# Layer 1 of a four-layer graph network: the next layers' weights are loaded and folded inside its first block, and the next block's first edge weights are written ahead of the evictions

## The chip, the cores and the metric

The kernel runs on one core of a Trainium2 chip. The metric is the device time of one execution in microseconds (us), as a median of runs. The profile is one further execution, taken by the hardware profiler; its times are counted from the first instruction of the span.

The engines are called PE (TensorE, matrix multiplication), DVE (VectorE), ACT (ScalarE), POOL (GpSimd) and SP (SyncE, which here only issues DMAs). DMAs are issued from SP, from ACT and from POOL.

## The reference

Four graph layers over the same 3327 nodes with 256 features and one dense 0/1 adjacency matrix. Each is followed by a residual and a layer norm. The change concerns layer 1 and its transition to layer 2:

```python
def _L1_gnn_ref(h, adj, W, a):
    Wh = h @ W.T
    a1, a2 = (a[:F_out], a[F_out:])
    s1 = Wh @ a1
    s2 = Wh @ a2
    e = jax.nn.leaky_relu(s1[:, None] + s2[None, :], negative_slope=LEAKY_SLOPE)
    e = jnp.where(adj == 0, NEG_INF, e)
    attention = jax.nn.softmax(e, axis=1)
    return attention @ Wh
...
x = _layernorm(x + _L0_gnn_ref(x, adj, ...), axis=-1)
x = _layernorm(x + _L1_gnn_ref(x, adj, L1_gnn_W, L1_gnn_a), axis=-1)
x = _layernorm(x + _L2_gnn_ref(x, adj, L2_gnn_W_fc, L2_gnn_b_fc, L2_gnn_w_att, L2_gnn_b_att), axis=-1)
x = _layernorm(x + _L3_gnn_ref(L3_gnn_t, x, adj, L3_gnn_W1, ...), axis=-1)
```

Layer 2 is a layer of the same kind without the leaky step, and with a bias. Layer 3 is two layers of four heads each (here l3a and l3b).

## The kernel before

**Tiles and blocks.** The nodes are 26 tiles of 128 rows (the last has 127). The target nodes are dealt into four blocks of 7, 7, 6 and 6 tiles. A layer walks over the blocks b, and in each block over all 26 source tiles j. For each j it needs the transposed adjacency of tile j against the block (`at_i`, 128 x 896 int32, 448 KB, in the first two blocks), the features of tile j (`feat`) and the edge weights `e` (L1629: max(rate, q) * adjacency, one DVE instruction). Then PE multiplies `e` with `feat` into one PSUM bank for each target tile of the block (L1723, seven matmuls a step, 257 columns: 256 sums and the softmax's denominator). Seven of the eight banks are accumulators; bank 7 serves everything else (projections, transposes).

**Layer 1, a step.** `adjacent` (L1644) takes the adjacency tile that was asked for, copies it as bf16 on ACT (L1656) and stores the copy in memory (`at_d`, from ACT's queue), for the layers 2 and 3, which read it back. The `at_i` and the `e` tiles share one set of 8 buffers (`edges`), the bf16 copies have 3 (`links`). In the first block, `ask` requests the adjacency tile of j + 3, and `fetch` the features of j + 3 (the first 20 tiles' features were stored earlier and are loaded again).

**Side work.** `pending` holds generators whose pieces are worked off between the steps (`work_off`): the end of layer 0 and the projection of its last six tiles for layer 1 in the first block; in later blocks the layer norm of the block just finished and its projection for layer 2 (`prepare`). In the steps of the first block in which projections take place, ACT works for them between two adjacency copies.

**End of a block.** For each bank DVE computes `inv` (reciprocal of the denominator, L1744) and `h` (sum times `inv` plus the residual, L1745). These are the evictions: a bank can only be used by the next block after its own. At the end of block 0 of layer 1 the layer 2 object is made, and with it its weights are loaded (`l2w`, two attention rows, the bias) and folded: `dots` multiplies each half of the weight with a row (L164) and reduces it (L165), which gives the extra columns for the attention terms. The l3a object is made after all of layer 1 in the code.

**What sets the order.** PE's order is that of the code in all layers. SP's is that of the code until the end of block 0 of layer 1 (`sp_order`). The order of DVE, ACT and POOL is that of the code until the end of the matmuls of block 0 (`in_order.close()` comes before the evictions); from there on a scheduler places the instructions by its own estimate. It drew the loads and folds of l3a up to the end of block 0. From l3a's layers on, PE, DVE and ACT are in the order of the code again.

Of the kernel before, what the change touches and what calls it, by code (L numbers as in the profile page):

```python
# [8 lines left out]
F32 = mybir.dt.float32  # L9
# [5 lines left out]
ALU = mybir.AluOpType  # L15
# [4 lines left out]
P = 128  # L20
# [30 lines left out]
def gat_stack(  # L51
# [105 lines left out]
        nc.sync.dma_start(t, src.rearrange("(c p) -> p c", p=P))  # L157
        return t

    def dots(work, dst, weight, row, nh):  # L160

        for c in range(kc):
            t = work.tile([P, dim], F32, tag="spread", name="dots", bufs=4)
            nc.vector.tensor_mul(t, weight[:, c, :dim], row)  # L164
            nc.vector.tensor_reduce(  # L165
                dst[:, c, :], t.rearrange("p (h d) -> p h d", h=nh), axis=AX.X, op=ALU.add
            )

    def attend(it, prob, proj, pool, psum, acc, col, width, copies):

# [1335 lines left out]
    def layers(rs, early=0, rest=None):  # L1506
# [23 lines left out]
        class Layer:  # L1530


            def __init__(self, name, slot, nh, leaky, load, bias=None, rate_d=None):
                self.slot, self.nh, self.leaky, self.bias = slot, nh, leaky, bias
                self.extra = 2 * nh if leaky else nh
                self.rate_d = rate_d
                if name == "l1":

                    self.weight = w1
                else:  # L1540
                    self.weight = work.tile(
                        [P, kc, dim + self.extra], F32, tag="weight", name=name + "w"
                    )
                    row_src, row_dst = load(self.weight)
                    dots(work, self.weight[:, :, dim : dim + nh], self.weight, row_dst, nh)
                    if leaky:
                        dots(work, self.weight[:, :, dim + nh :], self.weight, row_src, nh)
                self.feat = [None] * nt
                self.rate = [None] * len(blocks)

            def project(self, j, ht, banks):

# [91 lines left out]
        def adjacent(j, b, first=False):  # L1644

            pn = rows_of(j)
            c0, c1 = cols_of(blocks[b])
            w = c1 - c0
            at = links.tile([P, wide], BF16, tag="at", name="at")
            if not first:  # L1650
                copy_rows(nc.sync, at[:pn, :w], at_d[j * P : j * P + pn, c0:c1])
                return at
            if (j, b) not in asked:
                ask(j, b)
            at_i = asked.pop((j, b))
            nc.scalar.copy(at[:pn, :w], at_i[:pn, :w])  # L1656
            copy_rows(nc.scalar, at_d[j * P : j * P + pn, c0:c1], at[:pn, :w])
            return at_i
# [36 lines left out]
        def work_off(steps=1):  # L1695
            while steps and pending:
                if next(pending[0], pending) is pending:
                    pending.pop(0)
                else:
                    steps -= 1  # L1700

        def work_until(done):
            while not done():
                assert pending
                work_off()

        def one_head(layer, nxt, banks_next):

            for b, block in enumerate(blocks):
                work_until(lambda: not layer.leaky or layer.rate[b] is not None)  # L1710
                accs = [bank(s) for s in range(len(block))]
                for j in range(nt):
                    pj = rows_of(j)
                    work_until(lambda: layer.feat[j] is not None)
                    at = adjacent(j, b, layer is l1)
                    if layer.leaky:
                        e = layer.weigh(j, b, at, 0)
                    for s, it in enumerate(block):
                        pn = rows_of(it)
                        for part in range(1 if layer.leaky else 3):  # L1720
                            f = layer.feat[j] if layer.leaky else layer.feat[j][:, part, :]
                            a = e if layer.leaky else at
                            nc.tensor.matmul(  # L1723
                                accs[s][:pn, : dim + 1],
                                a[:pj, s * P : s * P + pn],
                                f[:pj, : dim + 1],
                                start=(j == 0 and part == 0),
                                stop=(j == nt - 1 and (layer.leaky or part == 2)),
                            )
                    if layer is l1 and b == 0:  # L1730
                        work_off(2 if j > 10 else 1)
                        if j + 3 < nt:
                            ask(j + 3, b)
                        fetch([j + 3])
                        if j > early and late:
                            l1.load_rates(late.pop(0))
                    elif j >= LATER:
                        work_off()
                work_until(lambda: not pending)
                in_order.close()  # L1740
                for s, it in enumerate(block):
                    pn = rows_of(it)
                    inv = small.tile([P, 1], F32, tag="inv", name="inv")
                    nc.vector.reciprocal(inv[:pn], accs[s][:pn, dim : dim + 1])  # L1744
                    nc.vector.scalar_tensor_tensor(  # L1745
                        h[it][:pn], accs[s][:pn, :dim], inv[:pn], h[it][:pn],
                        op0=ALU.mult, op1=ALU.add,
                    )
                if b == 0:
                    nxt = nxt()  # L1750
                    sp_order.close()
                pending.append(prepare(nxt, b, banks_next, normed=False))

        def many_heads(layer, nxt, finish):

# [236 lines left out]
        def load_plain(w, row_src, row_dst):  # L1992
            def load(t):
                nc.sync.dma_start(t[:, :, :dim], w.rearrange("(c p) f -> p c f", p=P))
                return load_row(work, row_src, "src", "spread"), load_row(work, row_dst, "dst", "spread")

            return load
# [59 lines left out]
        made = []  # L2057

        def second():
            made.append(  # L2060
                Layer(
                    "l2", "g", 1, False, load_plain(l2_w, l2_att[:dim], l2_att[dim:]),
                    load_row(work, l2_b, "bias"),
                )
            )
            return made[0]

        one_head(l1, second, (7,))
        l2 = made[0]
        l3a = Layer("l3a", "f", heads, True, load_heads(l3_w1, l3_a1), rate_d=rate3_d[0])  # L2070
        one_head(l2, lambda: l3a, (7,))
        rs.enter_context(
            tc.manual_schedule(
                engines={
# [2 lines left out]
            )  # L2077
        )
        l3b = Layer("l3b", "g", heads, True, load_heads(l3_w2, l3_a2), rate_d=rate3_d[1])
        many_heads(l3a, l3b, finish_hidden)  # L2080
        many_heads(l3b, None, finish_last)
        work_until(lambda: not pending)
# [81 lines left out]
```

## Time and profile before

| | us |
|---|---|
| runs, median of 3 | 3398.66 (3390.78 to 3407.27) |
| profiled execution | 2952.55 |
| its span | 2950.7 |

The stretches of the span, with the busy time of the engines and the TensorE clock that was granted (1 is full speed):

| stretch, us | what | PE | DVE | ACT | clock |
|---|---|---|---|---|---|
| 0 to 1367 | layer 0, features of 20 tiles for layer 1 | 778.51 | 1012.14 | 549.36 | 0.74 |
| 1367 to 1460 | layer 1, block 0 | 87.36 | 36.67 | 31.56 | 1.00 |
| 1460 to 1469 | the boundary | 2.30 | 7.90 | 2.81 | 0.69 |
| 1469 to 1548 | layer 1, most of block 1 | 78.91 | 44.51 | 33.50 | 0.99 |
| 1548 to 1622 | end of block 1, most of block 2 | 74.00 | 42.04 | 29.62 | 1.00 |
| 1622 to 1694 | end of block 2, most of block 3 | 71.41 | 41.41 | 30.07 | 1.00 |
| 1694 to 1971 | end of layer 1, layer 2 | 270.48 | 45.69 | 42.58 | 0.99 |
| 1971 to 2455 | layer 3, first part | 480.68 | 448.70 | 58.14 | 0.99 |
| 2455 to 2951 | layer 3, second part | 473.35 | 455.66 | 74.80 | 0.98 |

A busy time close to the length of the stretch means that this engine has hardly any idle time there. The times of PE are partly modelled by the profiler, as are the ends of its matmuls. Two matmul records stand for one float32 matmul.

### The profile page before, as it was taken

To read this page: it belongs to the slowest core of one execution; us is meant where nothing else is said; L and a number is where in the kernel's file an instruction comes from. 1 tells how busy PE (TensorE), PEld (TensorE's weight loads), DVE (VectorE), ACT (ScalarE), POOL (GpSimd) and SP (SyncE) were. 2 spreads that over 40 slices of the span, in tenths; PEclk is the share of its full clock that TensorE was granted. 3 is DMA by queue.
4 is the path that set the end of the run, shared out by engine and by line. 5 is a ranking of instruction groups with operands and counts; after the bars stand their busy time and mean duration, and the time that the engine had idled before them with its cause. 6 is when DMAs were issued, how large, how long until landed. Compare 5 with 4: busy or idle time off the path is not lost.

```text
span 2950.7 us, 45073 instructions
## 1 busy us (share of the span) xinstructions
PE 2317.0 (79%) x15862; PEld 1359.2 (46%) x15862; DVE 2134.7 (72%) x5615; ACT 852.4 (29%) x2381; POOL 992.3 (34%) x1061
## 2 busy tenths in 40 slices
PE   7466667556545416657899999999999999999997
PEld 4222323222222103325688888763546567534332
DVE  6789789968776518755455521138999999999997
ACT  3244445434334304533344411110010110111211
POOL 2676767777777777772000000000000000000000
PEclk8576777777767757889999999999999999999998
DMA  7685655545644435545776733331222222212211
GB/s 234 194 263 147 187 166 171 141 130 158 166 112 114 112 107 124 171 120 165 227 208 195 201 82 107 110 98 45 73 61 84 75 80 63 73 43 62 59 47 48
DMA packets 183854, 370.50 MB, mean 126 GB/s; under 512 B 35772, under 2 KB 124707, under 8 KB 182596
## 3 DMA queue, kind: packets, MB, share of 16 engines
q1 hardware_dynamic: 103994, 178.49, 21.4%
q0 software_dynamic: 51008, 155.70, 19.1%
q10 hardware_dynamic: 28618, 33.33, 3.3%
q8 instruction: 128, 2.10, 0.3%
q14 instruction: 106, 0.87, 0.1%
HBM read 327.52 MB, written 46.23 MB: 127 GB/s over the span
## 4 chain that ended last, share of the span: by engine, by line
PE 46%; DVE 4%; DMA 2%; issue 0%; ACT 0%; SPq 0%; DVEq 0%; POOL 0%; POOLq 0%; ACTq 0%
PE acc L1773 18%; PE acc L1723 16%; PE acc L1781 9%; DVE e L1629 3%; PE misc L1557 3%; DMA at<-at_d 1%; PE misc L1666 0%; DMA at_d<-at 0%; DMA at_i<-in_adj_t_dram 0%; DVE stats L1952 0%; DVE h L1950 0%; DVE h L1745 0%; DVE both L1947 0%; PE misc L1822 0%; DMA dst<-in_l_att_dram 0%
## 5 line engine op out<-in xcount | busy, mean ns | idle before, releaser
L912 POOL DMA_INDIRECT g<-table_d,lst x894 | 851.6, 953 | 273.1 <-issue 245.6
L1629 DVE SCALAR_TENSOR_TENSOR e<-rate,feat,at 128x896 f32<-128x896 f32 (+4 forms) x832 | 843.6, 1080 | 59.2 <-PE acc L1781 47.7
L1015 PE MATMUL acc<-g,ident 128*128 128x512 f32 (+1 forms) x896 | 505.5, 708 | 262.3 <-ACT g L1012 246.1
L1773 PE MATMUL acc<-e,feat 128*32 128x384 f32 (+2 forms) x6656 | 692.7, 515 | 6.7 <-DVE h L1745 4.2
L1773 PEld LDWEIGHTS acc<-e,feat 128*32 128x32 f32 x6656 | 307.1, 110 | 300.2 <-issue 161.5
L1015 PEld LDWEIGHTS acc<-g,ident 128*128 128x128 f32 x896 | 195.1, 228 | 481.6 <-ACT g L1012 364.6
L1781 PE MATMUL acc<-e,feat 128*32 128x384 f32 (+3 forms) x3328 | 383.3, 512 | 0.0
L1012 ACT ACTIVATE g<-g,w 128x256 f32<-128x256 f32 x883 | 365.4, 495 | 0.4 <-ACT minus L489 0.4
L932 DVE TENSOR_TENSOR y<-g,minus_ps 128x1028 f32<-128x1028 f32 (+2 forms) x233 | 273.4, 1173 | 125.0 <-DMA g<-table_d,lst 115.9
L938 DVE SCALAR_TENSOR_TENSOR y<-y,a_ps 128x257 f32<-128x257 f32 x894 | 324.3, 418 | 24.8 <-PE a_ps L781 6.2
L1723 PE MATMUL acc<-feat,e 128*128 128x257 f32 (+2 forms) x1352 | 303.5, 382 | 9.1 <-DVE inv L1744 6.4
L1723 PEld LDWEIGHTS acc<-feat,e 128*128 128x128 f32 (+2 forms) x1352 | 254.9, 191 | 46.9 <-issue 9.3
L1723 PE MATMUL acc<-feat,at 128*128 128x257 bf16 (+2 forms) x2028 | 237.9, 274 | 4.2 <-DMA at<-at_d 4.0
L1781 PEld LDWEIGHTS acc<-e,feat 128*32 128x32 f32 (+1 forms) x3328 | 162.0, 110 | 130.8 <-issue 88.1
L1723 PEld LDWEIGHTS <-at 128*128 128x128 bf16 (+2 forms) x2028 | 198.8, 99 | 38.0 <-DMA at<-at_d 4.5
L553 PE MATMUL v<-code,leads 65*128 65x512 bf16 (+1 forms) x182 | 83.1, 458 | 156.9 <-DVE cand L579 111.0
L1629 DVE SCALAR_TENSOR_TENSOR e<-rate,feat,at_i 128x896 f32<-128x896 f32 (+2 forms) x104 | 112.3, 1081 | 92.1 <-DMA at_i<-in_adj_t_dram 44.6
L579 DVE MAX8 cand<-v 128x8 f32<-128x104 f32 (+2 forms) x858 | 158.9, 260 | 21.7 <-PE v L556 21.7
L1609 POOL DMA_DIRECT2D rate3b_d<-rate_rows x4 | 2.1, 520 | 449.8 <-ACT rate_rows L1608 449.8
L251 POOL TENSOR_TENSOR rstds<-rstds,minus_half 128x7 f32<-128x7 f32 (+1 forms) x8 | 12.0, 1506 | 385.0 <-DVE rstds L250 385.0
L1959 POOL TENSOR_TENSOR rstds<-rstds,minus_half 128x7 f32<-128x7 f32 (+1 forms) x4 | 7.6, 1912 | 384.5 <-DVE rstds L1958 384.5
L1656 ACT CAST at<-at_i 128x896 bf16<-128x896 int32 (+2 forms) x104 | 92.1, 885 | 111.9 <-DMA at_i<-in_adj_t_dram 75.5
(253 smaller groups left out, 1864.6 us busy)
## 6 DMA issues: line engine op xcount, KB each, us to landing
adj_i<-in_adj_dram SPq DMA_DIRECT2D x75, 512.0 KB
at<-at_d SPq DMA_DIRECT2D x150, 224.0 KB
at_i<-in_adj_t_dram SPq DMA_DIRECT2D x50, 448.0 KB
at<-at_d SPq DMA_DIRECT2D x75, 192.0 KB
at<-at_d SPq DMA_DIRECT2D x75, 191.8 KB
g<-table_d,lst POOLq DMA_INDIRECT x894, 2.8
at_d<-at ACTq DMA_DIRECT2D x50, 224.0 KB
at_i<-in_adj_t_dram SPq DMA_DIRECT2D x25, 384.0 KB
```

Of the source, the lines that this page charges most:

```text
L579: nc.vector.max(spread[:, c0 + c, :], view(v[:, :w]))
L912: nc.gpsimd.indirect_dma_start(out=g[:, k - k0, :], out_offset=None, in_=table_d[:, :], in_offset=bass.IndirectOffsetOnAxis(ap=entry["lst" ...
L932: nc.vector.tensor_tensor(y, rows, minus_src[:, None, :].to_broadcast([P, m, dim + 1]), op=ALU.max)
L938: nc.vector.scalar_tensor_tensor(y, y, 1.0, a_ps[:, : dim + 1], op0=ALU.mult, op1=ALU.mult, accum_out=sc)
L1012: nc.scalar.activation(rows, rows, AF.Copy, scale=w[:, k : k + 1])
L1015: nc.tensor.matmul(dst, ident, rows, start=start, stop=stop)
L1557: nc.tensor.matmul(pacc[:pn, : dim + self.extra], ht[:, k, :pn], self.weight[:, k, :], start=(k == 0), stop=(k == kc - 1),)
L1629: nc.vector.scalar_tensor_tensor(e[:pn, : c1 - c0], self.rate[b][:pn, h_of, : c1 - c0], q, at[:pn, : c1 - c0], op0=ALU.max, op1=ALU.mult,)
L1656: nc.scalar.copy(at[:pn, :w], at_i[:pn, :w])
L1723: nc.tensor.matmul(accs[s][:pn, : dim + 1], a[:pj, s * P : s * P + pn], f[:pj, : dim + 1], start=(j == 0 and part == 0), stop=(j == nt - 1 ...
L1773: nc.tensor.matmul(accs[x][p][q : q + 32, : hi - lo], f[:pj, at0 : at0 + 32], es[at0 // hd][:pj, lo:hi], start=(j == 0), stop=(j == nt - 1),)
L1781: nc.tensor.matmul(accs[x][pairs][h_of * 32 : (h_of + 1) * 32, : hi - lo], f[:pj, dim + h_of : dim + h_of + 1].to_broadcast([pj, 32]), es[ ...
```

## The change

Three things are changed.

1. `dots` does one half of a weight in a call; a layer's constructor only loads (`self.rows = load(...)`), and a new method `fold` returns the steps of the fold as a list: 2 for l2, 4 for l3a.
2. `one_head` is given a table of layers to make, by step: in block 0 of layer 1, l2 is made after step 9 and l3a after step 15. Each layer's fold steps are done one a step, from 4 steps later on: steps 13 and 14 for l2, 19 to 22 for l3a.
3. At the end of each of layer 1's blocks but the last, the edge weights of the next block for j = 0 and 1 are requested and computed (`ready`) before the evictions in the code. `in_order.close()` now comes after the evictions of block 0.

l3b is still loaded and folded after layer 2, and layers 2 and 3 stand in the code as before.

```diff
-    def dots(work, dst, weight, row, nh):
-
-        for c in range(kc):
-            t = work.tile([P, dim], F32, tag="spread", name="dots", bufs=4)
-            nc.vector.tensor_mul(t, weight[:, c, :dim], row)
-            nc.vector.tensor_reduce(
-                dst[:, c, :], t.rearrange("p (h d) -> p h d", h=nh), axis=AX.X, op=ALU.add
-            )
+    def dots(work, dst, weight, row, nh, c):
+
+        t = work.tile([P, dim], F32, tag="spread", name="dots", bufs=4)
+        nc.vector.tensor_mul(t, weight[:, c, :dim], row)
+        nc.vector.tensor_reduce(
+            dst[:, c, :], t.rearrange("p (h d) -> p h d", h=nh), axis=AX.X, op=ALU.add
+        )
...
-                    row_src, row_dst = load(self.weight)
-                    dots(work, self.weight[:, :, dim : dim + nh], self.weight, row_dst, nh)
-                    if leaky:
-                        dots(work, self.weight[:, :, dim + nh :], self.weight, row_src, nh)
+                    self.rows = load(self.weight)
...
+            def fold(self):
+
+                w, nh = self.weight, self.nh
+                row_src, row_dst = self.rows
+                steps = [(w[:, :, dim : dim + nh], row_dst, c) for c in range(kc)]
+                if self.leaky:
+                    steps += [(w[:, :, dim + nh :], row_src, c) for c in range(kc)]
+                return [lambda s=s: dots(work, s[0], w, s[1], nh, s[2]) for s in steps]
...
-        def one_head(layer, nxt, banks_next):
+        def one_head(layer, make, banks_next):
+
+            folds, ready = [], {}
+
+            def fetched(j, b):
+                at = adjacent(j, b, layer is l1)
+                return at, layer.weigh(j, b, at, 0) if layer.leaky else None
...
-                    at = adjacent(j, b, layer is l1)
-                    if layer.leaky:
-                        e = layer.weigh(j, b, at, 0)
+                    at, e = ready.pop(j) if j in ready else fetched(j, b)
...
+                    if b == 0 and j in make:
+                        made.append(make[j]())
+                        folds += [(j + 4 + i, step) for i, step in enumerate(made[-1].fold())]
+                    while folds and folds[0][0] <= j:
+                        folds.pop(0)[1]()
                 work_until(lambda: not pending)
-                in_order.close()
+                assert not folds
+                if layer is l1 and b + 1 < len(blocks):
+                    work_until(lambda: layer.rate[b + 1] is not None)
+                    for j in range(2):
+                        ready[j] = fetched(j, b + 1)
                 for s, it in enumerate(block):
...
                 if b == 0:
-                    nxt = nxt()
+                    in_order.close()
                     sp_order.close()
-                pending.append(prepare(nxt, b, banks_next, normed=False))
+                pending.append(prepare(made[0] if layer is l1 else made[1], b, banks_next, normed=False))
...
-        one_head(l1, second, (7,))
-        l2 = made[0]
-        l3a = Layer("l3a", "f", heads, True, load_heads(l3_w1, l3_a1), rate_d=rate3_d[0])
-        one_head(l2, lambda: l3a, (7,))
+        def third():
+            return Layer("l3a", "f", heads, True, load_heads(l3_w1, l3_a1), rate_d=rate3_d[0])
+
+        one_head(l1, {9: second, 15: third}, (7,))
+        l2, l3a = made
+        one_head(l2, {}, (7,))
...
         l3b = Layer("l3b", "g", heads, True, load_heads(l3_w2, l3_a2), rate_d=rate3_d[1])
+        for step in l3b.fold():
+            step()
```

More of the change, by code (lines that the diff above doesn't have):

```diff
@@ L2059, in second @@
         def second():
[L2060 to L2064, printed above, removed]
-            )
-            return made[0]
-        one_head(l1, second, (7,))
-        l2 = made[0]
-        l3a = Layer("l3a", "f", heads, True, load_heads(l3_w1, l3_a1), rate_d=rate3_d[0])
-        one_head(l2, lambda: l3a, (7,))
+            return Layer(
+                "l2", "g", 1, False, load_plain(l2_w, l2_att[:dim], l2_att[dim:]),
+                load_row(work, l2_b, "bias"),
+            )
+        def third():
[3 more added lines that the diff above has]
+        one_head(l2, {}, (7,))
         rs.enter_context(
```

## The prediction

> Times are us of the profiled execution's clock unless I say otherwise. at_i(k), c(k) and e(k) are the adjacency tile k of a block, its bf16 copy on ScalarE and its edge weights on VectorE; "evictions" are the pairs `inv`, `h` (L1744, L1745).
>
> **What bounds the kernel now.** The page first: TensorE is busy most of the span, and the chain that ended last is matmuls.
>
> ```profile
> span 2950.7 us, 45073 instructions
> ...
> PE 2317.0 (79%) x15862; PEld 1359.2 (46%) x15862; DVE 2134.7 (72%) x5615; ACT 852.4 (29%) x2381; POOL 992.3 (34%) x1061
> ...
> PE 46%; DVE 4%; DMA 2%; issue 0%; ACT 0%; SPq 0%; DVEq 0%; POOL 0%; POOLq 0%; ACTq 0%
> ```
>
> The change touches layer 1 only, so next the busy time by stretch: its first block, the boundary, its second block. Columns after the duration: busy PE, PEld, DVE, ACT, POOL, then the granted clock, DMA share, GB/s.
>
> ```profile
> 1367.00:1460.00 93.00, 87.36 (x402) 74.21 (x402) 36.67 (x57) 31.56 (x58) 4.63 (x6) 1.00 0.76 243
> 1460.00:1469.00 9.00, 2.30 (x6) 1.01 (x4) 7.90 (x20) 2.81 (x3) 0.00 (x0) 0.69 0.81 259
> 1469.00:1548.00 79.00, 78.91 (x368) 69.00 (x369) 44.51 (x81) 33.50 (x60) 1.50 (x1) 0.99 0.71 208
> ```
>
> Both blocks are TensorE's; only the 9 us between them are not (2.30 busy). TensorE's waits from 1460 to 1700 say that this is the one stall of the rest of the layer:
>
> ```profile
> PE acc L1723 <- DVE inv L1744: 6.4, 1, 6.4
> PE acc L1723 <- DVE h L1745: 1.0, 2, 0.6
> ```
>
> The first waits for VectorE to empty bank 0. VectorE's timeline shows why it was late (idle before an instruction and its releaser in brackets):
>
> ```profile
> 1456.13 0.76 DVE L164 TENSOR_TENSOR dots<-l2w,dst 128x256 f32<-128x256 f32 x2 [4.33 <-DMA dst<-in_l_att_dram]
> 1456.80 0.74 DVE L165 TENSOR_REDUCE l2w<-dots 128x1 f32<-128x256 f32 x2
> 1457.46 1.15 DVE L1629 SCALAR_TENSOR_TENSOR e<-rate,feat,at_i 128x896 f32<-128x896 f32 x1
> 1461.06 1.15 DVE L1629 SCALAR_TENSOR_TENSOR e<-rate,feat,at_i 128x896 f32<-128x896 f32 x1 [2.46 <-DMA at_i<-in_adj_t_dram]
> 1462.13 0.75 DVE L164 TENSOR_TENSOR dots<-l3aw,dst 128x256 f32<-128x256 f32 x2
> 1462.81 0.73 DVE L165 TENSOR_REDUCE l3aw<-dots 128x4 f32<-128x256 f32 x2
> 1463.46 0.75 DVE L164 TENSOR_TENSOR dots<-l3aw,src 128x256 f32<-128x256 f32 x2
> 1464.13 0.41 DVE L165 TENSOR_REDUCE l3aw<-dots 128x4 f32<-128x256 f32 x1
> 1464.46 1.14 DVE L1629 SCALAR_TENSOR_TENSOR e<-rate,feat,at_i 128x896 f32<-128x896 f32 x1
> 1465.52 0.41 DVE L165 TENSOR_REDUCE l3aw<-dots 128x4 f32<-128x256 f32 x1
> 1465.84 0.16 DVE L1744 RECIPROCAL inv<-acc 128x1 f32<-128x1 f32 x1
> ```
>
> TensorE's block 0 ends at 1460.25; the first eviction starts 5.6 later, behind the folds of both later weights and e(0) to e(2). In all, the boundary costs 8.8: at 1480.32 TensorE had done 26 matmuls of block 1, each 0.434 (3.04 a step of seven), so it stands as if it had begun at 1480.32 - 26 x 0.434 = 1469.0. More than 8.8 the boundary cannot give: 0.3% of the span.
>
> [...] So an eviction waits for whatever the waiting instruction ahead of it waits for; the lines above agree (fold and e(1) held `inv` while both its inputs were there). [...] at_i(0), issued at 1450.80 beside 1.15 MB of later weights, was copied at 1457.23 (6.4); at_i(1) to (3), issued at 1456.23, 1458.67, 1462.29, took 4.8, 4.5 and 3.6. [...]
>
> ```profile
> 1466.60:1469.00 2.40, 2.05 (x4) 1.01 (x4) 2.40 (x7) 0.21 (x1) 0.00 (x0) 0.50 0.96 270
> 1469.00:1472.00 3.00, 2.90 (x11) 2.54 (x12) 3.00 (x10) 1.88 (x2) 0.00 (x0) 0.79 0.64 243
> ```
>
> **The change part by part.**
>
> *Weights loaded at j = 9.* SP gets four more DMAs (bias, l2w, src, dst: 128 + 256 + 128 + 128 KB) between feat(12), issued at 1394.84, and at_i(13), issued at 1396.58. At the block's 243 GB/s the 0.65 MB take 2.7; issue adds 4 x 0.4 = 1.6, and dst now waits for a DMA of ScalarE to finish, at most some 3. at_i(13) thus comes 4 to 7 later. Who needs it: e(13), done at 1403.1 before, which TensorE needs at 1411.94: cover 8.9; and c(13), on ScalarE's queue ahead of the projection's activations, at 1412.41. Cost 0; were the delay 12, it would cost 3.
>
> *Weights loaded at j = 15.* 512 KB behind feat(18) (SP at 1413.76); SP's next issue was at 1418.56 and here a step takes 5.18, because TensorE also projects. Transfer 2.1, issue 1.6: inside SP's 4.8 of idle time. Cost 0; uncovered, at most 2.
>
> *Six folds inside block 0.* Each is one multiply (0.42) and one reduce (0.41): 5.0 in all. They stand behind e(13), e(14) and e(19) to e(22), where VectorE idles 4.0 a step until 1435, then 1.2 to 5.1. One waits for the row of rates to have been stored, over at 1435.6, before VectorE gets there. Cost 0, uncovered 5.0.
>
> *Folds gone from the boundary.* 1.4 + 2.6 of VectorE, the second on the path, and 1.15 MB less beside at_i(0) and at_i(1).
>
> *Edge weights ahead of the evictions.* The code asks for two. The order of the built program has four: e(0) e(1) e(2) e(3), then `inv`, `h` of bank 0. This is the new wait, and behind it are all seven evictions, for which TensorE waits. Their tiles share 8 buffers. By the addresses in the build, at_i(2) takes at_i(0)'s buffer and at_i(3) takes at_i(1)'s, so at_i(3) cannot be asked for before e(1) and c(1). The chain, with durations of the trace:
> - c(25) starts at 1452.3 as before (c(22) at 1447.8 waited for a store of at_d, and that store and the next ones are not touched), ends 1453.2. at_i(1) takes tile 25's buffer: asked for then, lands 3.6 later, 1456.8.
> - e(1): 1456.8 to 1458.0. at_i(3) asked for, lands at 1461.6. e(3) ends at 1462.8.
> - So the first eviction starts at 1462.8 against 1465.84: 3.0 gained.
> - Behind it the order is worse. Before: seven evictions with one e and one `stats`, 4.88 from the first `inv` to the last `h`. After: four `stats`, four aggregates and two e, e(4) and e(5), stand between them. With start-to-start steps from the trace (inv to h 0.20, h to inv 0.39, inv to e 0.10, e to h 1.05, inv to aggregate to `stats` 0.19, `stats` to h 0.34) I get 7.5. The last bank is free at 1470.3, against 1470.72 before.
>
> TensorE's first step of block 1 ends with the last bank: gain 0.4. Its idle stretch shrinks from 6.4 to some 3.2[...], so part of the half-speed stretch (0.9 in the 8.8) may go: 0 to 0.9, I take half. Sum: -0.9, say **-1 us**.
>
> *Later boundaries.* In the built order VectorE's rows between blocks 1 and 2, and 2 and 3, are the same as before, with e's ahead of evictions already (at 1556 TensorE does not stall); TensorE's and GpSimd's whole orders are unchanged. Cost 0; a bound is the 1.0 of the second wait above. Inside block 1 ScalarE's `turned` copy stands one cast later, covered by the 3.0 step before its projection.
>
> The profiled execution took 2952.55 (1.85 around its span); minus 1 is 2951.5. The median of the runs is 3398.66, 446 more, and no view here shows where. [...] I carry the difference unscaled: 3397.6.
>
> **Rivals.**
> *A, forecast:* the evictions queue behind e(3); -1, 3397.6; own range -4 to +2. Chance 0.50.
> *B, the stall goes:* at_i(1) and (3) land before TensorE is done, the evictions follow TensorE at once. For it: 1.15 MB fewer in flight there. Against it: the shared buffers. Worth 8.8 less the 1.5 that seven evictions (some 4.5) take over a step of 3.04: -7, 3391.6. Chance 0.22.
> *C, slower:* same place, longer transfers. Two links in series are in front of the evictions, so each us of latency costs 2. Break-even is at 3.6 + 0.4/2 = 3.8; at at_i(0)'s 6.4 it is 2 x 2.8 - 0.4 = +5, 3403.9. For it: 4.5 and 4.8 were also seen; against it: those stood beside the weights. Chance 0.20.
> *D, the change does not act there:* the unseen state of the timed runs, or a stall in block 0 that I called covered, decides; either sign, 10 to 20. Chance 0.08.
>
> **How the numbers follow.** This kernel's three runs lie 0.49% apart, so 0.5%, 17 us, is about what can be told from no change; A, B and C all lie inside it, and only noise or D carries a median out. Faster: 0.03 of A, 0.06 of B, 0.04 of D: 0.13. Slower: 0.03 of A, 0.02 of C, 0.04 of D: 0.09. Same: 0.78. The range takes B and C and the runs' half spread of 8 to 10: 3380 to 3413.
>
> **What would show it.** In the changed profile: the folds in block 0 with no wait of TensorE there; at the boundary four e's, the fourth with idle time before it that ends with at_i, then `inv`; TensorE's wait for `inv` of some 3 instead of 6.4, but more waits for `h`, and its 26th matmul of block 1 within 2 of the same place. Wrong if `inv` starts before 1460 plus 1 (B), or after 1465.8 (C), or if TensorE waits in block 0.

## The result, and the profile after

| | us |
|---|---|
| before, median of 12 runs | 3395.66 (3379.50 to 3410.72) |
| after, median of 12 runs | 3397.14 (3382.78 to 3410.57) |
| ratio, with its 95% interval | 1.0002 (0.9981 to 1.0022) |
| profiled execution of after | 3405.73, its span 3403.9 |

No change that can be measured. A second set of runs of the two kernels gave a ratio of 1.0005 (0.9991 to 1.0019).

In some sets of runs layer 0 takes some 450 longer than in others, for every kernel of the set; the first profile of the kernel before comes from a short one, its timed runs and the first profile of the kernel after from long ones (more at the end). From the start of layer 1 on the times agree within the spread of layer 2 (given below), so all comparisons below are of stages of layer 1, and ratios come only from runs made beside each other.

From the page of the kernel after, the lines that answer to those shown of before:

```profile
span 3403.9 us, 45049 instructions
...
PE 2387.4 (70%) x15841; PEld 1377.2 (40%) x15862; DVE 2147.6 (63%) x5615; ACT 856.1 (25%) x2381; POOL 992.0 (29%) x1061
...
PE 39%; DVE 4%; DMA 2%; issue 1%; ACT 1%; ACTq 0%; DVEq 0%; POOL 0%; SPq 0%; POOLq 0%
```

All shares are smaller because layer 0 is longer. The stretches of layer 1 say more: block 0, the boundary, the second block. Columns after the duration: busy PE, PEld, DVE, ACT, POOL, then clock, DMA share, GB/s.

```profile
1816.00:1909.00 93.00, 87.58 (x402) 74.15 (x402) 41.70 (x66) 33.44 (x60) 4.63 (x6) 1.00 0.82 255
1909.00:1918.00 9.00, 4.31 (x11) 2.17 (x11) 6.88 (x25) 2.82 (x3) 0.00 (x0) 0.80 0.76 235
1918.00:1997.00 79.00, 78.63 (x364) 68.14 (x364) 40.91 (x67) 32.36 (x58) 1.50 (x1) 0.98 0.65 196
```

In block 0 VectorE works 5.0 more (41.70 against 36.67) in the same 93 us: the folds lie there, and TensorE does not notice. At the boundary TensorE starts earlier than before, in small pieces. Its timeline (start, duration, in brackets the wait before it and its releaser, x126 is the number of matmul records merged into a line):

```profile
1881.44 27.57 PE L1732 MATMUL acc<-feat,e 128*128 128x257 f32 x126
1913.06 0.67 PE L1732 MATMUL acc<-feat,e 128*128 128x257 f32 x2 [4.05 <-DVE inv L1762]
1913.90 2.04 PE L1732 MATMUL acc<-feat,e 128*128 128x257 f32 x4 [0.17 <-DVE mvs L242]
1916.27 2.91 PE L1732 MATMUL acc<-feat,e 128*128 128x257 f32 x6 [0.32 <-DVE inv L1762]
1919.55 25.77 PE L1732 MATMUL acc<-feat,e 128*128 128x257 f32 x114 [0.37 <-DVE h L1763]
1945.16 0.38 PE L1671 MATMUL misc<-ident,h 128*128 128x128 f32 x2
```

Block 0 ends at 1881.44 + 27.57 = 1909.01. The wait for the first bank is 4.05 instead of 6.4, but the first transposes of block 1, nine steps later, start 1945.16 - 1909.01 = 36.15 behind it, against 35.94 in the first profile of before. This distance is called *the boundary* below. Nine steps alone take 27.57 (the first line is nine steps of block 0, seven matmuls each, so its 126 records are two a matmul), so 8.6 of it is loss, as before. VectorE shows why (L1762 is `inv`, L1763 `h` in this kernel):

```profile
1905.60 1.15 DVE L1634 SCALAR_TENSOR_TENSOR e<-rate,feat,at_i 128x896 f32<-128x896 f32 x1 [4.37 <-DMA at_i<-in_adj_t_dram]
1907.93 1.15 DVE L1634 SCALAR_TENSOR_TENSOR e<-rate,feat,at_i 128x896 f32<-128x896 f32 x1 [1.18 <-DMA at_i<-in_adj_t_dram]
1911.17 1.15 DVE L1634 SCALAR_TENSOR_TENSOR e<-rate,feat,at_i 128x896 f32<-128x896 f32 x1 [2.08 <-DMA at_i<-in_adj_t_dram]
1912.23 0.16 DVE L1762 RECIPROCAL inv<-acc 128x1 f32<-128x1 f32 x1
...
1914.60 1.13 DVE L1634 SCALAR_TENSOR_TENSOR e<-rate,feat,at_i 128x896 f32<-128x896 f32 x1
...
1917.89 1.12 DVE L1634 SCALAR_TENSOR_TENSOR e<-rate,feat,at_i 128x896 f32<-128x896 f32 x1
1918.93 0.47 DVE L1763 SCALAR_TENSOR_TENSOR h<-acc,inv,h 128x256 f32<-128x256 f32 x1
```

The first three lines are e(1), e(2), e(3), each waiting for its adjacency tile; the first eviction stands behind e(3), 3.22 after block 0's end; e(4) and e(5) stand among the evictions, and the last ends at 1919.40, 10.39 after block 0's end. Before it was 10.47.

### The profile page after: what moved, and what is told of

It reads as the page before. It is cut to its first block, busy times and chain, and to the rows that moved or that the text cites. A ratio compares the mean times of both kernels' runs of the same rounds, so it can differ in the third digit from the quotient of the medians.

```text
span 3403.9 us, 45049 instructions
## 1 busy us (share of the span) xinstructions
PE 2387.4 (70%) x15841; PEld 1377.2 (40%) x15862; DVE 2147.6 (63%) x5615; ACT 856.1 (25%) x2381; POOL 992.0 (29%) x1061
## 5 line engine op out<-in xcount | busy, mean ns | idle before, releaser
L1014 PE MATMUL acc<-g,ident 128*128 128x512 f32 (+1 forms) x896 | 560.4, 769 | 412.2 <-ACT g L1011 349.0
L1014 PEld LDWEIGHTS acc<-g,ident 128*128 128x128 f32 x896 | 209.0, 246 | 665.7 <-ACT g L1011 426.6
L578 DVE MAX8 cand<-v 128x8 f32<-128x104 f32 (+2 forms) x858 | 168.3, 261 | 114.7 <-issue 74.2
L552 PEld LDWEIGHTS <-leads 65*128 65x128 bf16 x182 | 22.7, 124 | 288.6 <-issue 85.3
L250 POOL TENSOR_TENSOR rstds<-rstds,minus_half 128x7 f32<-128x7 f32 (+1 forms) x8 | 12.1, 1507 | 385.6 <-DVE rstds L249 385.6
```

Of the source, the lines that this page charges most:

```text
L552: nc.tensor.matmul(v[:, :w], leads[:, b, :], code[:, :w], start=True, stop=False)
L578: nc.vector.max(spread[:, c0 + c, :], view(v[:, :w]))
L1014: nc.tensor.matmul(dst, ident, rows, start=start, stop=stop)
```

## The experiments

None of these kernels leaves any computation out. All figures are from one profile each; those with a sign are us before (-) or behind (+) the end of the last matmul of block 0. "Loss" is the boundary less 27.57 (the prediction's 8.8 for the kernel before is counted to the end of the 26th matmul of block 1 instead).

| kernel | block 0 | first `inv` | last `h` ends | boundary | loss |
|---|---|---|---|---|---|
| before | 93.13 | +5.59 | +10.47 | 35.94 | 8.4 |
| before, again | 93.00 | +5.41 | +10.29 | 37.24 | 9.7 |
| after | 93.04 | +3.22 | +10.39 | 36.15 | 8.6 |
| after, again | 92.89 | +3.99 | +11.16 | 36.08 | 8.5 |
| folds_only | 92.69 | +4.27 | +8.70 | 34.80 | 7.2 |
| ready_only | 93.40 | +3.69 | +12.05 | 36.97 | 9.4 |
| no_ready | 92.85 | +3.84 | +11.01 | 35.93 | 8.4 |
| hold2 | 93.61 | -2.32 | +3.45 | 28.37 | 0.8 |
| hold4 | 92.64 | -1.33 | +2.91 | 27.83 | 0.3 |
| hold4, timed | 93.46 | -0.68 | +3.56 | 28.49 | 0.9 |
| hold4_noready | 92.91 | -2.56 | +1.69 | 31.96 | 4.4 |
| hold4_nofolds | 92.77 | -1.52 | +2.72 | 30.10 | 2.5 |
| loads_together | 96.28 | +2.85 | +10.70 | 36.61 | 9.0 |
| loads_first | 102.62 | +4.21 | +11.41 | 36.33 | 8.8 |

From the first transposes to the start of layer 2 every one of them takes 209.0 to 209.6: what a boundary gains or loses is not given back in layer 1. Layer 2 took 265.3 to 272.0 in no relation to the edits, and the rest of the span, from layer 3's first matmul with edge weights on, 976.9 to 977.8.

**1. The kernel before, again.** No edit.

> The kernel before, profiled once more. The first profile of it had a span of 2950.7 while all its timed runs took 3380 to 3411; that of the kernel after had 3403.9, with all of the difference in layer 0 (layer 1 began at 1367 and at 1816). If layer 0 simply went differently in that one execution, this profile has a span of 3385 to 3415, layer 1 begins at 1805 to 1825, and the boundary (end of block 0's matmuls to the first transposes of h0) is 35.9 +- 0.3 as in the first profile. If the change made layer 0 slower when profiled, the span is near 2951 again.

Measured: span 2951.3, layer 1 from 1361.89. The first expectation of the span missed. The other, that the change makes layer 0 slower, falls with the next runs: folds_only and hold4, which have the change, began layer 1 at 1367.66 and 1363.10 in this same set. The length goes with the set of runs. The boundary was 37.24, not 35.9 +- 0.3: the evictions are as in the first profile (+10.29 against +10.47), and the rest is clock. TensorE was still at half speed after all banks were free, which they were at 1465.18:

```profile
1463.00:1466.00 3.00, 2.62 (x7) 2.01 (x7) 3.00 (x10) 1.88 (x2) 0.00 (x0) 0.50 0.78 300
1466.00:1468.00 2.00, 2.00 (x7) 1.60 (x6) 2.00 (x10) 0.00 (x0) 0.00 (x0) 0.56 0.32 117
```

The boundary of one kernel thus moves by up to 1.3 from one execution to the next.

**2. The folds alone.** The kernel after without the early edge weights, the written order ending as before:

```diff
                 assert not folds
-                if layer is l1 and b + 1 < len(blocks):
-                    work_until(lambda: layer.rate[b + 1] is not None)
-                    for j in range(2):
-                        ready[j] = fetched(j, b + 1)
+                in_order.close()
...
                 if b == 0:
-                    in_order.close()
                     sp_order.close()
```

> The weights and folds in block 0 as in the kernel after; no early edge weights, and the written order ends ahead of the evictions as before. Built order: e(0) to e(3), then the seven evictions close together with e(4) among them and the statistics behind. Queue theory (the boundary is what stands on VectorE ahead of and between the evictions): first eviction 3.2 after block 0's last matmul as in the kernel after, the evictions take some 5.4 instead of 7.2, boundary 34.4 (36.15 after, 35.94 before). Transfer theory (the edge weights' tiles set it, whatever stands between the evictions): 36.0 to 36.4.

Measured: boundary 34.80. VectorE, from e(3) on:

```profile
1463.56 1.15 DVE L1634 SCALAR_TENSOR_TENSOR e<-rate,feat,at_i 128x896 f32<-128x896 f32 x1 [1.82 <-DMA at_i<-in_adj_t_dram]
1464.62 0.23 DVE L1759 RECIPROCAL inv<-acc 128x1 f32<-128x1 f32 x2
...
1467.13 1.14 DVE L1634 SCALAR_TENSOR_TENSOR e<-rate,feat,at_i 128x896 f32<-128x896 f32 x1
1468.18 0.87 DVE L1760 SCALAR_TENSOR_TENSOR h<-acc,inv,h 128x256 f32<-128x256 f32 x2
```

e(3) is in front here as well, waiting for at_i(3); the tile came later than in the kernel after (first `inv` +4.27 against +3.22). But with one edge weight among the evictions and no statistics they take 4.4 instead of 7.2, and the boundary is 1.3 shorter. That fits the queue theory (34.4), in which what stands between the evictions counts, better than the transfer theory (36.0 to 36.4). One profile each, against a spread of 1.3: the direction is as expected, the size not secured.

**3. The early edge weights alone.** The kernel before with the lines removed above put into it, and `in_order.close()` behind the evictions; the weights are made there too.

```diff
...
                 work_until(lambda: not pending)
-                in_order.close()
+                if layer is l1 and b + 1 < len(blocks):
+                    work_until(lambda: layer.rate[b + 1] is not None)
+                    for j in range(2):
+                        ready[j] = fetched(j, b + 1)
...
                 if b == 0:
+                    in_order.close()
                     nxt = nxt()
```

> The two early edge weights and the later end of the written order alone; the weights are made and folded at the boundary as before. Built order: e(0), e(1), two folds of layer 2's weight, e(2), then evictions with statistics, aggregates, e(3), e(4) among them; layer 3's folds behind them. Queue theory: first eviction at 2 to 6 after block 0's end, then some 7.5 for the evictions: boundary 35 to 39, 37 as the likeliest, no gain. If asking for the edge weights early is what helps: 33 or less.

Measured: boundary 36.97, TensorE waiting 6.6 for `inv` in four pieces; 37 was the likeliest value. The first eviction comes earlier than before (+3.69 against +5.4), the last later (+12.05 against +10.3). So neither half of the change brings the evictions close to block 0's end.

**4. The written order kept longer.** The kernel after with VectorE, ScalarE, GpSimd and SP kept to the order of the code until step 4 of block 1 (around the boundary SP issues nothing but adjacency tiles, in the kernel after and here):

```diff
+                    if layer is l1 and b == 1 and j == 4:
+                        in_order.close()
+                        sp_order.close()
...
-                if b == 0:
-                    in_order.close()
-                    sp_order.close()
```

> The kernel after with the written order of VectorE and ScalarE kept until step 4 of block 1. Built order: e(0), e(1), then the seven evictions with nothing between them, then e(2) to e(4), then the statistics. Queue theory: at_i(1) lands 3.4 before block 0 ends, so the first eviction follows the last matmul by 0.3, the last ends 4.5 later, e(2) and e(3) still come before TensorE's steps 2 and 3: boundary 28 to 30, span 7 shorter from block 0 on. Transfer theory: TensorE waits for e(2) or e(4) instead, since at_i(4) takes the buffer of at_i(2): boundary 33 to 36. Clock theory (half clock after the idle stretch is most of the cost): the stretch goes, so as the queue theory, but the clock stays at 1.00 all through.

Measured: boundary 27.83. VectorE at the boundary, and TensorE without one listed wait from the end of block 0's side work to the first transposes:

```profile
1453.34 1.15 DVE L1634 SCALAR_TENSOR_TENSOR e<-rate,feat,at_i 128x896 f32<-128x896 f32 x1 [4.62 <-DMA at_i<-in_adj_t_dram]
1454.41 0.16 DVE L1765 RECIPROCAL inv<-acc 128x1 f32<-128x1 f32 x1
...
1458.17 0.48 DVE L1766 SCALAR_TENSOR_TENSOR h<-acc,inv,h 128x256 f32<-128x256 f32 x1
1458.57 3.45 DVE L1634 SCALAR_TENSOR_TENSOR e<-rate,feat,at_i 128x896 f32<-128x896 f32 x3
```

```profile
1428.17 55.57 PE L1732 MATMUL acc<-feat,e 128*128 128x257 f32 x252
1483.57 0.38 PE L1671 MATMUL misc<-ident,h 128*128 128x128 f32 x2
```

The first eviction starts 1.33 before block 0's last matmul ends (1455.74), and not 0.3 behind it as expected, because bank 0 is finished six matmuls, some 2.6, ahead of the last one. e(2) to e(4), three in a row behind the evictions, are all in time. The transfer theory (a wait for e(2) or e(4) instead) falls. The clock (third figure from the right) stays at 1.00, so the half-speed stretch was a consequence of the stall:

```profile
1456.00:1462.00 6.00, 6.00 (x26) 4.24 (x25) 5.81 (x13) 2.46 (x3) 0.00 (x0) 1.00 0.72 228
1462.00:1541.00 79.00, 79.00 (x373) 69.09 (x372) 42.63 (x78) 34.07 (x61) 1.50 (x1) 1.00 0.70 214
```

**5. The same, timed.**

> The version of hold4 (written order of VectorE and ScalarE kept until step 4 of block 1), timed. In its profile the boundary lasted 27.8 against 35.9 and 37.2 in two profiles of the kernel before. Queue theory: that is 8 to 9 less a run, so 0.24% to 0.32% faster, ratio 0.997, at the edge of what runs spread over 0.5 to 1% can show. Rival (given back later: layers 2 and 3 are bound by something that starts at a fixed time): ratio 1.000, and in the profile the time from the first transposes of h0 to the end is longer by what was gained.

Measured: 2940.09 (median of 7) against 2950.18 (median of 11) for the kernel before beside it: ratio 0.9962 (0.9948 to 0.9976), 10 us faster. The boundaries of two profiles each account for 7.5 to 9.4 of it (35.94 and 37.24 against 27.83 and 28.49). Its interval lies below those of the kernel after against before. Nothing was given back: from the first transposes to the end of the span it took 1454.1, against 1454.5 and 1459.2 in the two profiles of the kernel before.

**6. The order kept until step 2.** As 4, with `j == 2`.

> The same with the written order kept until step 2 only. Built order: e(0), e(1), then the seven evictions with statistics and aggregates between them but no edge weight; e(2) behind them. Tells e(2) and e(3) ahead of the first eviction from what stands between the evictions. Queue theory: first eviction as in hold4, some 1.3 before the last matmul of block 0; evictions some 7.2 instead of 4.2; boundary 30 to 31. If only the first eviction's start counts: 28.

Measured: 28.37. VectorE's first `inv`, last `h` and e(2), where block 0 ends at 1456.07:

```profile
1453.75 0.16 DVE L1765 RECIPROCAL inv<-acc 128x1 f32<-128x1 f32 x1
...
1459.05 0.47 DVE L1766 SCALAR_TENSOR_TENSOR h<-acc,inv,h 128x256 f32<-128x256 f32 x1
1459.43 1.14 DVE L1634 SCALAR_TENSOR_TENSOR e<-rate,feat,at_i 128x896 f32<-128x896 f32 x1
```

The evictions took 5.77, not 7.2. The estimate of 30 to 31 was too high because it took over the duration of the kernel after, in which e(4) and e(5) stand among the evictions, 1.05 from start to start. With statistics alone between them the last bank is free at +3.45. TensorE uses bank 6 for the first time 2.6 after its start, so only 0.8 is lost. The statistics lengthen the evictions by 1.5 (5.77 against 4.24 in hold4), but the loss is no larger than in hold4's two profiles (0.8 against 0.3 and 0.9), since they began earlier. By its number alone this run fits the rival, that only the start of the first eviction counts (28). Two others speak against that: folds_only began its evictions later than the kernel after (+4.27 against +3.22) and had the shorter boundary, and ready_only began them earlier than the kernel before (+3.69 against +5.59 and +5.41) and had no shorter one (36.97 against 35.94 and 37.24). From the kernel after to this one, the first eviction moved forward by 5.5 and the evictions became 1.4 shorter. So of the kernel after's loss most is e(2) and e(3) in front of the first eviction, and next e(4) and e(5) among them.

**7. and 8. The cover of the loads.** The kernel after with both weights loaded at steps 9 and 10, and at steps 0 and 1:

```diff
-        one_head(l1, {9: second, 15: third}, (7,))
+        one_head(l1, {9: second, 10: third}, (7,))
...
-        one_head(l1, {9: second, 15: third}, (7,))
+        one_head(l1, {0: second, 1: third}, (7,))
```

> The kernel after with both later weights loaded one after the other, at steps 9 and 10 of block 0, folds right behind: 1.16 MB and nine more issues on SP ahead of at_i(14) instead of 0.65 MB ahead of at_i(13). Prediction's working (a delay of 4 to 7 for 0.65 MB inside a cover of 8.9): delay 8 to 13, so block 0 lasts 93.0 plus 0 to 4; 94 as the value. If transfers there have no effect on TensorE at all: 92.6 to 93.2. Boundary as in the kernel after, 36 to 37.5.

> The kernel after with the weights loaded at steps 0 and 1, where edge weights and rows of features come in only just in time (VectorE idle 2.5 to 3.6 for feat in steps 1 to 3). No cover there: each load delays at_i or feat by 3 to 7, block 0 lasts 95 to 102 instead of 93.0, with TensorE waiting for e in steps 2 to 5. If the position of the loads does not matter: 92.6 to 93.2.

Measured: block 0 lasts 96.28, inside the expected 93 to 97, and 102.62, just above 95 to 102. In loads_together TensorE's timeline has the loss at one place:

```profile
1403.77 0.69 PE L1671 MATMUL misc<-ident,h 128*128 128x128 f32 x2 [2.55 <-ACT columns L1589]
1404.25 4.65 PE L1732 MATMUL acc<-feat,e 128*128 128x257 f32 x14
```

This wait is 0.83 in every other step of that kind, and the 14 matmul records take 3.20 elsewhere: 1.72 of waiting and 1.45 of half clock behind it (0.53 from 1403.70 to 1405.00, 0.50 from there to 1407.00, 0.95 from there to 1409.00). What came late was ScalarE, not an edge weight: its queue stood behind the store of an adjacency copy, which was issued 4.0 after the copy had ended. The releaser named is the load of layer 3's weight; what held the store itself is not shown.

```profile
1397.62 0.94 ACT L1661 CAST at<-at_i 128x896 bf16<-128x896 int32 x1
1402.59 0.34 ACTq L135 DMA_DIRECT2D at_d<-at  x1
1402.98 0.17 ACT L1571 ACTIVATE feat<-misc 128x1 f32<-128x1 f32 x1 [4.42 <-DMA l3aw<-in_l_w_dram]
```

In loads_first TensorE waits twice for edge weights, whose features came late:

```profile
1378.00 4.99 PE L1732 MATMUL acc<-feat,e 128*128 128x257 f32 x14 [4.31 <-DVE e L1634]
1385.07 20.15 PE L1732 MATMUL acc<-feat,e 128*128 128x257 f32 x84 [2.08 <-DVE e L1634]
```

So the loads are not free in themselves; at steps 9 and 15, six steps apart, they are covered.

**9. The kernel after, again.**

> The kernel after, profiled and timed once more beside the kernel before. Queue theory: the boundary again 36.1 (its first profile) to 37; over many boundaries no gain: ratio 0.998 to 1.001. If the 446 us between the two first profiles belonged to the place or time of the run and not to the kernel, this profile begins layer 1 at 1360 to 1370, not at 1816.

Measured: ratio 1.0005 (0.9991 to 1.0019), boundary 36.08. Layer 1 began at 1820.52: the long layer 0 was there again, for all four kernels of this set.

**10. Without the early edge weights.** As 2, but with `in_order.close()` left behind the evictions.

> The kernel after without the two early edge weights; the later weights in block 0 and the written order ending behind the evictions stay. In the built program all five engines have the order of the kernel after: e(0) to e(3) are put ahead of the evictions anyway. So boundary as in after_again within 0.7. If asking early matters in itself: 2 or more longer.

Measured: 35.93. VectorE's e(1), e(2), e(3) and the first `inv`, where block 0 ends at 1920.32:

```profile
1917.50 1.15 DVE L1634 SCALAR_TENSOR_TENSOR e<-rate,feat,at_i 128x896 f32<-128x896 f32 x1 [4.54 <-DMA at_i<-in_adj_t_dram]
1919.96 1.15 DVE L1634 SCALAR_TENSOR_TENSOR e<-rate,feat,at_i 128x896 f32<-128x896 f32 x1 [1.32 <-PE acc L1732]
1923.09 1.15 DVE L1634 SCALAR_TENSOR_TENSOR e<-rate,feat,at_i 128x896 f32<-128x896 f32 x1 [1.97 <-DMA at_i<-in_adj_t_dram]
1924.16 0.16 DVE L1758 RECIPROCAL inv<-acc 128x1 f32<-128x1 f32 x1
```

The lines that ask for e(0) and e(1) ahead change nothing as long as the scheduler is free behind them: it puts four edge weights there with or without these lines. What differs between 2 and this kernel is only where the written order ends.

**11. The kept order without the early edge weights.** As 4, without the `ready` lines.

> hold4 without the early edge weights: VectorE's order is then the seven evictions and behind them e(0), e(1), ... Tells what having e(0) and e(1) ahead is worth once the evictions are not late. Worked out: evictions start as bank 0 is finished, 2.5 before block 0's last matmul, the last ends 1.7 behind it, e(0) ends at 2.8, TensorE stands still for 2.8: boundary 30.4, against 27.8 and 28.5 in two profiles of hold4.

Measured: 31.96. The evictions ran as worked out (-2.56 to +1.69), and TensorE waited 2.89 for e(0). The 1.5 more than expected is clock: TensorE's timeline from the wait to the transposes, and the windows there.

```profile
1919.64 29.23 PE L1732 MATMUL acc<-feat,e 128*128 128x257 f32 x126 [2.89 <-DVE e L1634]
1948.70 0.38 PE L1671 MATMUL misc<-ident,h 128*128 128x128 f32 x2
```

```profile
1916.70:1919.60 2.90, 0.04 (x1) 0.00 (x0) 2.79 (x8) 1.05 (x2) 0.00 (x0) 1.00 0.58 216
1919.60:1921.00 1.40, 1.36 (x4) 1.16 (x5) 1.40 (x2) 0.00 (x0) 0.00 (x0) 0.69 0.56 109
1921.00:1922.50 1.50, 1.50 (x5) 1.22 (x4) 1.50 (x2) 0.00 (x0) 0.00 (x0) 0.50 0.66 249
1922.50:1924.00 1.50, 1.50 (x6) 1.18 (x5) 0.93 (x2) 0.85 (x1) 0.00 (x0) 0.65 0.01 2
```

**12. The kept order without the moved loads and folds.** As 3, with the order kept until step 4 as in 4.

> hold4 without the first half of the change: the later weights are loaded and folded at the boundary as in the kernel before, the early e(0), e(1) and the written order until step 4 stay. Built order: e(0), e(1), seven evictions, layer 2's folds, e(2), e(3), layer 3's folds, e(4). Queue theory (only what stands ahead of the last eviction counts, and the folds now have steps of 3.04 of TensorE's to lie in): boundary 28 to 29.5. If the weights' 1.15 MB beside at_i(1) to at_i(4) are what delays: 31 or more.

Measured: 30.10, between the two forecasts, so neither holds alone. The evictions are as in hold4 (+2.72); TensorE then waits 0.25 for e(5) and 1.59 for e(6). On VectorE these stand behind both weights' folds, the statistics and a part of the layer norm, and layer 3's folds had waited 1.23 for their attention row. So the folds cost something here not at the evictions but by pushing back what follows them. With the order kept, then, the early edge weights are worth some 3.5 to 4 (31.96 against 28.49 and 27.83) and the moved folds some 1.6 to 2.3 (30.10 against the same). Without the kept order the folds alone gave 1.1 to 2.4 (34.80 against 35.94 and 37.24) and the edge weights nothing. These are differences of single profiles, and two profiles of one kernel lay up to 1.3 apart.

## Why the prediction was right

The forecast was -1 us, 3397.6 in runs; measured 3397.14, and a boundary that is 0.2 longer than in the first profile of before and 1.1 shorter than in the second. The runs show only that nothing changed by more than some 7 (0.2%). They cannot tell -1 from 0, and rival C would have given "no change" as well. The traces decide between the rivals: the first `inv` stands at +3.22 and +3.99, where B was to be earlier than +0.75 and C later than +5.55. So the place of the evictions was forecast rightly; that the time agrees to 0.5 is luck.

- *Loads and folds inside block 0, cost 0.* Shown: 93.04 and 92.89 against 93.13 and 93.00. The tile behind the first weights, at_i(13), was issued 3.7 later (1849.12 against 1396.58 + 448.8, the two starts of layer 1 being 448.8 apart), and e(13) ended 5.0 later (1856.88 against 1403.07 + 448.8), inside the cover of 8.9. The cover is real and finite: loads_together went through it and made block 0 3.2 to 3.3 longer than in the kernel before. The queue that ran out first was ScalarE's, the second of the two named, by a store and not by c(13), and not VectorE's e(13).
- *The four edge weights in front of the evictions, by the order of the build.* Shown. They, not the code's two lines, are the new wait (no_ready).
- *The chain through the shared buffer.* Shown in the trace of after, step by step. SP asked for at_i(1) at 1901.50 and for at_i(3) at 1906.82, when e(1) had just ended at 1906.75:

```profile
1901.50 0.34 SPq L135 DMA_DIRECT2D at_i<-in_adj_t_dram  x1
...
1906.82 0.33 SPq L135 DMA_DIRECT2D at_i<-in_adj_t_dram  x1
```

  The mis-sized term is the latency: 3.6 was taken for both tiles, they took 4.1 and 4.35 (landings at 1905.60 and 1911.17). With the first request 0.5 earlier than forecast, the first eviction stood at +3.22 instead of +2.55, and at +3.99 in the second profile. By the prediction's own break-even of 3.8 the two latencies should have cost some 0.9; the earlier request (0.5) and the next term (0.3) made up for it. That they cancelled is luck.
- *Evictions spread out.* Forecast 7.5 from the first `inv` to the last `h`; 7.17 in both profiles. The last bank was free at +10.39, forecast 1470.3 - 1460.25 = +10.05, before +10.47. Of the 0.4 forecast as gain 0.1 came, and none in the second pair of profiles (+11.16 against +10.29).
- *Half of the clock's stretch goes.* Not shown. The idle stretch was 4.05, not 3.2, and the clock fell to 0.50 as before (0.50 from 1916.20 to 1919.50). That part of the stretch goes at 3.2 was the author's guess: the trace of before shows at the boundary only what followed a wait of 6.4 (0.50, then 0.79, the two windows in the prediction). At 3.2 the clock might have fallen as well: in hold4_noready it fell to 0.50 behind a wait of 2.89.
- *Later boundaries, cost 0.* Shown: 209.39 from the first transposes to layer 2, as in the kernel before.
- *The 446 us between the profile and the median.* All of it is in layer 0: from the first transposes to the end of the span the long executions took 1458.7 and 1455.5 (after, after again), the short ones 1454.5 and 1459.2 (before, before again). The forecast did not depend on where it lies, since the difference was carried over whole.

One relation ties the profiles together, worked out from them: TensorE's loss is the time of the last `h` less 2.6, as long as no edge weight is later than that. The 2.6 is the time from TensorE's first use of a bank in a block to its first use of the last one, six matmuls of 0.434. It gives 0.8 (hold2), 0.3 (hold4), 1.0 (hold4 timed), 8.4 (no_ready), 8.6 (after again), 8.8 (loads_first) and 9.4 (ready_only), each within 0.1 of the table. It gives 7.9 for before, 6.1 for folds_only, 7.7 for before again, 7.8 for after and 8.1 for loads_together, where the table has 0.5, 1.1, 2.0, 0.8 and 0.9 more. In the first four of these five the windows give a half clock of 6.8, 6.8, 10.2 and 6.8 at the boundary, and in loads_together four matmul records took 2.05 there, against 1.03 elsewhere; the excess is put down to that. After again had 0.50 from 1918.20 to 1921.00 too, and in no_ready, loads_first and ready_only six records took 2.91, against 1.46 elsewhere; there it cost nothing. Rivals C and D did not come either: nothing in block 0 stalled, and of the longer transfers that C feared, 4.1 and 4.35 came instead of its 6.4. So the change took 4.0 of folds away from the time ahead of the first eviction, put e(3) with its tile's latency in their place, and spread the evictions out; the time of the last `h` stayed where it was, within 0.9. Rival B needed the evictions not to wait for e(3); in hold4, where e(2) and e(3) stand behind them, the stall goes as B had it.

## What to carry to other kernels

Where TensorE waits for a set of banks to be emptied, look at when the *last* one is emptied, less the time until it is first used (2.6 here): an earlier first eviction is worth nothing if the others are spread out behind it. Having the next block's first inputs written ahead pays only if the order is fixed as far as the point where it matters; a scheduler that is free right behind those lines put the same four instructions there with and without them, and the gain (ratio 0.9962, 0.9948 to 0.9976) came from fixing the order for four more steps. Work that is put ahead of a release on the same queue should be work whose inputs have already landed: here e(1)'s tile landed 3.4 before the end of block 0, that of e(3), which had to wait for a buffer, 2.2 after it.

## What was not expected of the hardware

- *Waits of 2.55 and 2.89 were followed by half of TensorE's clock.* The prediction hoped for less of it behind its wait of some 3.2. But behind the 2.55 in loads_together and the 2.89 in hold4_noready the clock was at 0.50 (from 1405.00 to 1407.00, and from 1921.00 to 1922.50), which cost 1.45 and 1.5 more, about half as much again as the wait itself. Behind the second wait of loads_first, 2.08, 84 matmul records took 20.15, against 18.47 in loads_together, so they were slowed too; behind the 1.59 in hold4_nofolds 42 records took 9.37, no longer than three times the 3.20 of 14 at full clock.
- *The half-speed stretch lasted 3.41, 6.83 and 10.24 in three profiles.* With the same evictions the clock was at 0.50 for 6.83 in the first profile of the kernel before (1463.46 to 1470.29) and for 10.24 in the second (1457.51 to 1467.75), and this cost 0.5 and 2.0; in hold4_noready it was 3.41 (1920.13 to 1923.55). The edges are worked out from the mean clocks of windows, and the three are two, three and one times 3.41.
- *Layer 0 has two lengths.* It ended at 1361 to 1368 in nine profiles and at 1816 to 1827 in five, for kernels that do not differ there; all profiles made beside each other had the same one. GpSimd's gathers of layer 0 (count, busy time and mean of one, then the idle time ahead of them) take as long in both, but wait longer in the long one. First the second profile of the kernel before, in the short one, then the second profile of the kernel after, in the long one:

```profile
L912 POOL DMA_INDIRECT g<-table_d,lst x894 | 852.7, 954 | 273.2 <-issue 243.1 <-PE acc L1015 10.2 <-DMA g<-table_d,lst 7.0
```

```profile
L911 POOL DMA_INDIRECT g<-table_d,lst x894 | 850.4, 951 | 399.5 <-issue 289.3 <-PE acc L1014 66.8 <-remote 33.0
```

  These waits explain 126 of the some 450; other waits of GpSimd in layer 0 are longer as well, those ahead of its stores of sums by 131 in the same two views (159.0 against 28.0). What makes the difference stays open, and no run here was made to tell. The later sets ran on three chips (the short ones on 13 and 3, the long one on 1), so the chip may be what decides. The kernel after was never profiled unedited in a set with the short layer 0, but its variants (folds_only, hold4, hold2 and others) were.
